# Sending a supertile's scatters as one group instead of through a paced queue, in a routed feed-forward kernel

## The chip, the cores and the metric

One Trainium2 chip, of which the kernel uses one core. Times are device microseconds (us) of one execution, from launch to end; the median over many runs is compared. The profile is one execution recorded by the hardware profiler.

## The reference

The input x holds 32 sequences of 256 tokens with 128 features, 8192 tokens in all. A modulation vector is made for each sequence from c and wmod, in six parts: shift, scale and gate for each of two halves. The two halves are:

```
h = layernorm(x) * (1 + ca) + sa
g = sigmoid(h Wg' + bg); a = sigmoid(h Wd' + bd); v = h Wv' + bv
s_t = a_t * s_(t-1) + (1 - a_t) * v_t          # scan along each sequence
x = x + ga * (s * g)

h = layernorm(x) * (1 + cb) + sb
p = softmax(h gate_w' + gate_b)                # 8 experts
y = sum over the two best experts e of p_e * (relu(h w1_e + b1_e) w2_e + b2_e)
x = x + gb * y
```

Each expert goes from 128 features to 512 and back to 128. All numbers are float32.

## The kernel before

The tokens are cut into 16 supertiles of 512 tokens (4 tiles of 128 tokens, two sequences). Each supertile passes four steps:

- `a_norm` (step 0): the first layer norm; ACT writes xn (L324).
- `a_mix` (step 1): transposes (px, L337), three matmuls of width 512 (pz, L346), the gates on ACT (ta L350, aa L352, tg L361), the scan on DVE (hs).
- `a_res` (step 2): transposes back (po, L374), the residual into xa, the second layer norm; ACT writes xm (L382).
- `a_route` (step 3): transposes (ph, L389), the logits (pl, L397), the rows back in token order (pb, L400), which ACT copies into rw (L402). DVE finds the two best experts, and a small matmul (pq, L423 and L425) counts the tokens that each expert has so far. From that DVE makes pi, the place of each of the 4 x 2 (tile, choice) pairs in a table of rows in HBM, reg. Each row has 130 words: the 128 features, the gate weight and the destination.

Eight indirect DMAs on POOL's queue (L447) write the rows of one supertile to reg, one for each pair of tile j and choice k, 128 rows each. In reg every expert has its own stretch, so that 256 rows in a row belong to one expert: a block. Reading and writing of reg is declared free of ordering between scatters, and between scatters and fills (`into_reg`).

After some supertiles (TAKE, and the last one) `table` computes on DVE which blocks are full by then: a table tb with the expert and the first row of each block. 45 blocks come from the nine tables of TAKE, the other 26 from the last table; 71 in all.

A block goes through these steps, each in another call of `b_step`:

- `b_load`: SyncE (SP) reads expert and row from tb into registers (L535, L536), loads the rows xr from reg (L538) and the expert's up-projection weights ww, 514 KB (L544). Blocks are loaded up to four ahead.
- `b_in`: two transposes (pbx, L551), and the split in a high part on ACT (xs, L553) and a low one on DVE (L554).
- `b_up`: twelve matmuls (L566 to L568) into p, and relu to hh on ACT (L574) or DVE (L572).
- `b_down`: a bias matmul (L584) and sixteen matmuls (L587) into pby, of which there is one PSUM buffer; ACT scales the result into yt (L591), eight buffers; two indirect DMAs on POOL's queue (L593) scatter it to yd.

At last `c_load` reads yd for a supertile on SP (L606), and `c_add` makes the gated sum on DVE (from L618) and stores the output (L623).

The order of the work is partly by hand. `steps` lists which steps of which supertiles stand beside each other (HEAD for the first supertiles); after each step, `between` calls `b_step` when more than BACK = 2 blocks are open and not begun. The framework's scheduler then orders the instructions of each engine, with the supertiles' steps raised in priority (AHEAD), and sets all semaphores. Each engine runs its queue in order.

In the kernel before the eight scatters of a supertile are not issued where they are made. They are appended to a list, `sending`, and `drip` takes one or two of them after each step and after each up-projection, in the order of the supertiles. Each one that is taken waits for the ACT instruction `behind`, which is the latest of the step, or the first relu of the up-projection. The blocks that a table opens are kept in `held` until the last scatter of their supertile has been taken. `b_load` has each row load wait for the last 16 scatters that were taken, and its register loads stand behind the previous block's weight load.

Of the kernel before, what the change touches and what calls it, by code (L numbers as in the profile page):

```python
# [15 lines left out]
AX = mybir.AxisListType  # L16
WAIT = mybir.DependencyInfo(mybir.DependencyClass.Sync, mybir.DependencyReason.DATA)

P = 128
# [35 lines left out]
def adaln_moe(ctx: ExitStack, tc: tile.TileContext, x, Wg, bg, Wv, bv, Wd, bd,  # L55
# [256 lines left out]
    def a_norm(s):  # L312
        g = LN1G.get(s, 0)
        if g:
            mv = wk.tile([P, g * T, 2], F32, tag=f"mva{g}", name=f"mva{s}")
            for i in range(g):
                stats(mv[:, i * T:(i + 1) * T], xa[:, s + i], f"a{s + i}")
            y, r = rsqrt(mv, f"a{s}", s)
            for i in range(g):
                ln1[s + i] = (y[:, i * T:(i + 1) * T], r[:, i * T:(i + 1) * T])  # L320
        y, r = ln1[s]
        xn = wk.tile([P, T, D], F32, tag="xn", name=f"xn{s}")
        for j in range(T):
            last = nc.scalar.activation(xn[:, j], xa[:, s, j], AF.Identity, scale=y[:, j], bias=r[:, j])  # L324
        return dict(s=s, xn=xn, last=last)

# [6 lines left out]
    def a_mix(a):  # L333
# [10 lines left out]
        for i in (2, 1, 0):  # L344
# [3 lines left out]
            if i == 2:  # L348
                ta = wk.tile([P, ST], F32, tag="ta", name=f"ta{s}")
                nc.scalar.activation(ta, z, AF.Tanh, scale=0.5, bias=hb[:, 2:3])  # L350
                aa = wk.tile([P, ST], F32, tag="aa", name=f"aa{s}")
                nc.scalar.activation(aa, ta, AF.Copy, scale=0.5, bias=0.5)  # L352
                for q in range(BPS):
                    w = slice(q * S, (q + 1) * S)
                    b = s * BPS + q
                    nc.vector.tensor_scalar(ta[:, w], ta[:, w], ngq[:, b:b + 1], gq[:, b:b + 1], op0=ALU.mult, op1=ALU.add)
            elif i == 1:
                nc.vector.scalar_tensor_tensor(ta, z, bvc, ta, op0=ALU.add, op1=ALU.mult)
            else:
                tg = wk.tile([P, ST], F32, tag="tg", name=f"tg{s}")  # L360
                a["last"] = nc.scalar.activation(tg, z, AF.Tanh, scale=0.5, bias=hb[:, 0:1])  # L361
        hs = wk.tile([P, ST], F32, tag="hs", name=f"hs{s}")
# [6 lines left out]
    def a_res(a):  # L369
# [11 lines left out]
        for j in range(T):  # L381
            a["last"] = nc.scalar.activation(xn[:, j], xt[:, j], AF.Identity, scale=y[:, j], bias=r[:, j])  # L382
        a["xn"] = xn

    def a_route(a, base):
# [13 lines left out]
        for j in range(T):  # L399
            nc.tensor.transpose(pb[:, j * P:(j + 1) * P], hT[:, j * P:(j + 1) * P], ident)  # L400
        rw = wk.tile([P, T, K, RW], F32, tag="rw", name=f"rw{s}", bufs=3)
        a["last"] = nc.scalar.activation(rw[:, :, :, 0:D], pb.rearrange("p (t d) -> p t d", d=D).unsqueeze(2).to_broadcast([P, T, K, D]), AF.Copy)  # L402
        lg = wk.tile([P, T, E], F32, tag="lg", name=f"lg{s}")
# [41 lines left out]
        nc.gpsimd.tensor_copy(rw[:, :, :, D + 1].bitcast(I32), dst[:, s * T:(s + 1) * T])  # L445
        def send(j, k):
            w = nc.gpsimd.indirect_dma_start(  # L447
                out=reg, out_offset=bass.IndirectOffsetOnAxis(ap=pi[:, j * K + k:j * K + k + 1], axis=0),
                in_=rw[:, j, k], in_offset=None)
# [7 lines left out]
    sending = []  # L457
    sent = []
    held = []
# [70 lines left out]

    loaded = []

    def b_load(n, tb, i):
        with tc.issue_after(loaded[-1].ins) if loaded else nullcontext():
            e = nc.sync.value_load(tb[i:i + 1, 0:1], min_val=0, max_val=E - 1)  # L535
            r = nc.sync.value_load(tb[i:i + 1, 1:2], min_val=0, max_val=E * CAP)  # L536
        xr = bk.tile([P, NJ, RW], F32, tag="xr", name=f"xr{n}", bufs=YTB + 6)
        w = nc.sync.dma_start(xr, reg[bass.ds(r, BLK)].rearrange("(t p) d -> p t d", p=P))  # L538
# [5 lines left out]
        loaded.append(nc.sync.dma_start(ww, wd[bass.ds(e, 1)].rearrange("o p f -> p (o f)")))  # L544
        return b
# [11 lines left out]
    def b_up(b):  # L557
        n, xs, ww = b["n"], b["xs"], b["ww"]
        hh = bk.tile([P, NH, BLK], F32, tag="hh", name=f"hh{n}")
        for k0 in range(0, NH, 2):  # L560
# [8 lines left out]
            for k in (k0, k0 + 1):  # L569
# [3 lines left out]
                else:  # L573
                    w = nc.scalar.activation(hh[:, k], p1[:, k - k0], AF.Relu, bias=bias)  # L574
                    b.setdefault("last", w)
        b["hh"] = hh
# [56 lines left out]
    def b_step():  # L633
# [23 lines left out]
    slot = 0  # L657
    alive = True

# [24 lines left out]
    for t, todo in enumerate(steps):  # L684
        def step3(s):
            nonlocal base, done
            with tc.high_priority(AHEAD[3] * (s >= EARLY)):
                base = a_route(st[s], base)
                if s in CLS:
# [3 lines left out]
                    counts.append(b)  # L693
                nb = len(blocks) + sum(len(x) for _, x in held)
                if s in TAKE:
                    n = full(s) - nb
                    tb, done = table(s, counts[:1] * (s > CUT) + [base], done, n, False)
                    held.append((s, [(tb, q, []) for q in range(n)]))
                elif s == NS - 1:
                    n = touched(s) - nb  # L700
                    tb, done = table(NS, counts, done, n, True)
                    fills(base)
                    rest = [(tb, q, []) for q in range(n)]
                    held.append((s, rest))
                    z = 0
                    for c in CLS:
                        u = max(E, touched(c) - nb) if c == CUT else touched(c) - nb
                        rest[u - 1][2].extend(range(z, c + 1))
                        z = c + 1
# [21 lines left out]
        if t == LATE:  # L731
            late_constants()
    alive = False
    while len(flow) < len(blocks) + 2 or ended or adding:
        b_step()
    assert not sending and not held

# [27 lines left out]
```

## Time and profile before

| | |
|---|---|
| median of 14 runs | 545.85 us (542.51 to 551.52) |
| the profiled execution | 549.71 us |
| its span, first to last instruction | 547.9 us |
| PE busy | 442.9 us, 2810 matmuls |
| ACT, DVE, POOL busy | 288.1, 283.3, 290.6 us |
| mean granted clock of TensorE | 0.866 |
| L447 on POOL | 128 instructions, 979 ns each |
| L593 on POOL | 142 instructions, 987 ns each |

PE is TensorE's matmuls, PEld its weight loads, DVE is VectorE, ACT ScalarE, POOL GpSimd, SP SyncE. A letter q behind the engine's name stands for its sequencer. A row of the timeline gives start, duration, engine, line, operation, the tiles written and read, how many instructions it merges, and in brackets the idle time of the engine before it and what ended it by the profile; "remote" is a semaphore whose sender the profile does not name, "issue" means that nothing it shows was waited for. A row of a stretch gives for each engine busy time and, behind x, the count of instructions. The ends of matmuls are modelled by the profiler. The granted clock is what TensorE's throttle let through, as a share of full speed.

### The profile page before, as it was taken

To read this page: it belongs to the slowest core of one execution; us is meant where nothing else is said; L and a number is where in the kernel's file an instruction comes from. 1 tells how busy PE (TensorE), PEld (TensorE's weight loads), DVE (VectorE), ACT (ScalarE), POOL (GpSimd) and SP (SyncE) were. 2 spreads that over 40 slices of the span, in tenths; PEclk is the share of its full clock that TensorE was granted. 3 is DMA by queue.
4 is the path that set the end of the run, shared out by engine and by line. 5 is a ranking of instruction groups with operands and counts; after the bars stand their busy time and mean duration, and the time that the engine had idled before them with its cause. 6 is when DMAs were issued, how large, how long until landed. Compare 5 with 4: busy or idle time off the path is not lost.

```text
span 547.9 us, 11399 instructions
## 1 busy us (share of the span) xinstructions
PE 442.9 (81%) x2810; PEld 370.7 (68%) x2810; DVE 283.3 (52%) x1511; ACT 288.1 (53%) x726; POOL 290.6 (53%) x322
## 2 busy tenths in 40 slices
PE   5668658679798799888978988776777999979991
PEld 3234415567677687756876977666676999979980
DVE  6999799568464673755547422311111220533464
ACT  4877346658555574746536533433333565636550
POOL 4537653355565566665555573666655254434451
PEclk9965586798797888988889786998979899979996
DMA  7993110826273444443442644456318676999974
GB/s 207 335 332 132 44 35 26 264 60 209 57 221 97 134 139 132 136 132 107 131 129 62 208 144 136 138 163 196 127 45 242 204 225 215 288 299 307 291 208 127
DMA packets 81845, 91.52 MB, mean 167 GB/s; under 512 B 8577, under 2 KB 66408, under 8 KB 81782
## 3 DMA queue, kind: packets, MB, share of 16 engines
q1 hardware_dynamic: 73024, 73.84, 45.9%
q0 software_dynamic: 8704, 16.94, 9.1%
q8 instruction: 26, 0.43, 0.3%
q14 instruction: 37, 0.30, 0.2%
q10 hardware_dynamic: 54, 0.02, 0.0%
HBM read 64.24 MB, written 27.43 MB: 167 GB/s over the span
## 4 chain that ended last, share of the span: by engine, by line
PE 63%; DVE 13%; issue 7%; DMA 5%; ACT 5%; another core or an unknown queue 3%; SPq 2%; POOL 1%; ACTq 0%; DVEq 0%; POOLq 0%
PE pby L587 26%; PE p L568 7%; PE p L566 6%; PE p L567 6%; PE pz L346 5%; PE pby L584 4%; PE pbx L551 3%; DVE sta L280 2%; PE pl L397 2%; DMA yk<-yd 1%; PE px L337 1%; PE po L374 1%; DVE hs L365 1%; ACT yt L591 1%
## 5 line engine op out<-in xcount | busy, mean ns | idle before, releaser
L593 POOL DMA_INDIRECT yd<-yt,xr x142 | 140.2, 987 | 141.6 <-ACT yt L591 105.8
L587 PE MATMUL pby<-wr,hh 128*128 x1136 | 167.9, 306 | 0.0
L447 POOL DMA_INDIRECT reg<-rw,pi x128 | 125.3, 979 | 76.2 <-issue 37.7
L587 PEld LDWEIGHTS pby<-wr,hh 128*128 128x128 f32 x1136 | 152.6, 214 | 10.0 <-issue 2.5
L574 ACT ACTIVATE hh<-p,ww 128x256 f32<-128x256 f32 x231 | 95.8, 480 | 39.4 <-issue 13.0
L591 ACT ACTIVATE yt<-pby,xr 128x128 f32<-128x128 f32 x142 | 44.9, 365 | 135.7 <-PE pby L587 55.7
L554 DVE TENSOR_TENSOR xs<-pbx,xs 128x256 fp32r<-128x256 f32 x71 | 30.0, 422 | 141.1 <-ACT xs L553 101.7
L566 PE MATMUL p<-xs,ww 128*128 128x256 f32 x284 | 92.2, 326 | 12.6 <-DVE hh L572 7.1
L567 PE MATMUL p<-xs,ww 128*128 128x256 f32 x284 | 83.5, 294 | 1.6 <-issue 1.5
L568 PE MATMUL p<-xs,ww 128*128 128x256 f32 x284 | 83.3, 294 | 1.5 <-issue 1.5
L566 PEld LDWEIGHTS p<-xs,ww 128*128 128x128 f32 x284 | 57.5, 203 | 14.5 <-DVE hh L572 7.9
L346 PE MATMUL pz<-h,wT 128*128 128x512 f32 x96 | 60.2, 749 | 7.0 <-ACT tg L361 4.2
L567 PEld LDWEIGHTS p<-xs,ww 128*128 128x128 f32 x284 | 57.5, 203 | 2.8 <-issue 2.8
L568 PEld LDWEIGHTS p<-xs,ww 128*128 128x128 f32 x284 | 57.0, 201 | 2.7 <-issue 2.7
L584 PE MATMUL pby<-b2w,ones_r 2*128 x71 | 28.5, 401 | 22.9 <-ACT yt L591 21.4
L584 PEld LDWEIGHTS pby<-b2w,ones_r 2*128 2x128 f32 x71 | 13.7, 193 | 41.1 <-ACT yt L591 24.8
L346 PEld LDWEIGHTS pz<-h,wT 128*128 128x128 f32 x96 | 20.2, 241 | 23.8 <-issue 10.0
L572 DVE TENSOR_SCALAR hh<-p,ww 128x256 f32<-128x256 f32 x53 | 25.4, 480 | 20.4 <-ACT hh L574 16.7
L551 PE MATMUL pbx<-ident,xr 128*128 128x128 f32 x142 | 30.5, 299 | 2.3 <-DMA xr<-reg 2.1
L553 ACT ACTIVATE xs<-pbx 128x256 fp32r<-128x256 f32 x71 | 27.5, 387 | 7.7 <-issue 2.3
L324 ACT ACTIVATE xn<-xa,nra,nya 128x128 f32<-128x128 f32 x64 | 26.5, 494 | 8.5 <-DVE nra L307 8.5
L382 ACT ACTIVATE xm<-xa,nrb,nyb 128x128 f32<-128x128 f32 x64 | 26.4, 484 | 4.4 <-DVE nrb L307 3.9
(181 smaller groups left out, 590.4 us busy)
## 6 DMA issues: line engine op xcount, KB each, us to landing
ww<-wd SPq DMA_DIRECT2D x71, 514.0 KB
xr<-reg SPq DMA_DIRECT2D x71, 130.0 KB
yk<-yd SPq DMA_DIRECT2D x30, 256.0 KB
wd<-wh SPq DMA_DIRECT2D x8, 514.0 KB
xa<-in_L_attn_x_dram SPq DMA_DIRECT2D x16, 256.0 KB
out_dram<-ot SPq DMA_DIRECT2D x15, 256.0 KB
yd<-yt,xr POOLq DMA_INDIRECT x142
w1s<-in_L_ffn_w_dram SPq DMA_DIRECT2D x8, 256.0 KB
```

What stands on the lines that cost most here:

```text
L346: nc.tensor.matmul(z, wT[:, i], h1, start=True, stop=True)
L447: w = nc.gpsimd.indirect_dma_start(out=reg, out_offset=bass.IndirectOffsetOnAxis(ap=pi[:, j * K + k:j * K + k + 1], axis=0), in_=rw[:, j, ...
L551: nc.tensor.transpose(px[:, j * P:(j + 1) * P], xr[:, j, 0:D], ident)
L554: nc.vector.tensor_tensor(xs[:, 1], px, xs[:, 0], op=ALU.subtract)
L566: nc.tensor.matmul(z, hi, xs[:, 0], start=True, stop=False)
L567: nc.tensor.matmul(z, hi, xs[:, 1], start=False, stop=False)
L568: nc.tensor.matmul(z, lo, xs[:, 0], start=False, stop=True)
L574: w = nc.scalar.activation(hh[:, k], p1[:, k - k0], AF.Relu, bias=bias)
L584: nc.tensor.matmul(py.rearrange("p (j d) -> p j d", d=D), ones_r, b2t, start=True, stop=False)
L587: nc.tensor.matmul(py[:, j * D:(j + 1) * D], hh[:, k, j * P:(j + 1) * P], we[:, k * D:(k + 1) * D], start=False, stop=(j == NJ - 1 and k = ...
L591: nc.scalar.activation(yt[:, j], py[:, j * D:(j + 1) * D], AF.Copy, scale=xr[:, j, D:D + 1])
L593: w = nc.gpsimd.indirect_dma_start(out=yd, out_offset=bass.IndirectOffsetOnAxis(ap=xr[:, j, D + 1:D + 2].bitcast(I32), axis=0), in_=yt[:, ...
```

## The change

The lists `sending`, `sent` and `held`, the function `drip` and the waits it sets are taken out. `a_route` issues its eight scatters itself, one after another. The blocks of a table go to `blocks` as soon as the table's instructions are written. A row load waits for scatters by the framework's own tracking of reg alone: for those that stand before it in the program. Its register loads may be moved ahead by the scheduler. The tiles rw and pi have two buffers instead of three. The arithmetic is the same, and so is the number of DMAs.

```diff
-        rw = wk.tile([P, T, K, RW], F32, tag="rw", name=f"rw{s}", bufs=3)
+        rw = wk.tile([P, T, K, RW], F32, tag="rw", name=f"rw{s}")
...
-        pi = wk.tile([P, T * K], I32, tag="pi", name=f"pi{s}", bufs=3)
+        pi = wk.tile([P, T * K], I32, tag="pi", name=f"pi{s}")
...
-        def send(j, k):
-            w = nc.gpsimd.indirect_dma_start(
-                out=reg, out_offset=bass.IndirectOffsetOnAxis(ap=pi[:, j * K + k:j * K + k + 1], axis=0),
-                in_=rw[:, j, k], in_offset=None)
-            into_reg(w.ins, "scat")
-            return w.ins
-
-        sending.extend((s, send, j, k) for j in range(T) for k in range(K))
+        for j in range(T):
+            for k in range(K):
+                w = nc.gpsimd.indirect_dma_start(
+                    out=reg, out_offset=bass.IndirectOffsetOnAxis(ap=pi[:, j * K + k:j * K + k + 1], axis=0),
+                    in_=rw[:, j, k], in_offset=None)
+                into_reg(w.ins, "scat")
...
-    def drip(n, behind):
-        for _ in range(min(n, len(sending))):
-            s, send, j, k = sending.pop(0)
-            w = send(j, k)
-            tc.add_manual_dep(w, behind.ins.name, WAIT, reason="pace of the rows on their way out")
-            sent.append(w)
-            if not sending or sending[0][0] != s:
-                while held and held[0][0] <= s:
-                    blocks.extend(held.pop(0)[1])
...
     def b_load(n, tb, i):
-        with tc.issue_after(loaded[-1].ins) if loaded else nullcontext():
-            e = nc.sync.value_load(tb[i:i + 1, 0:1], min_val=0, max_val=E - 1)
-            r = nc.sync.value_load(tb[i:i + 1, 1:2], min_val=0, max_val=E * CAP)
+        e = nc.sync.value_load(tb[i:i + 1, 0:1], min_val=0, max_val=E - 1)
+        r = nc.sync.value_load(tb[i:i + 1, 1:2], min_val=0, max_val=E * CAP)
...
-        for x in sent[-2 * K * T:]:
-            tc.add_manual_dep(w.ins, x.name, WAIT, reason="its rows")
...
         if i >= 1 and flow[i - 1]:
             b_up(flow[i - 1])
-            drip(1 if alive else 2, flow[i - 1]["last"])
...
-                    held.append((s, [(tb, q, []) for q in range(n)]))
+                    blocks.extend((tb, q, []) for q in range(n))
...
         for i, s in todo:
             (step0, step1, step2, step3)[i](s)
-            drip(2 if t < len(steps) - NS or len(sending) > K * T else 1, st[s]["last"])
             between()
```

More of the change, by code (lines that the diff above doesn't have):

```diff
@@ L1 @@
-from contextlib import ExitStack, nullcontext
+from contextlib import ExitStack
 import concourse.bass as bass
@@ L16 @@
 AX = mybir.AxisListType
-WAIT = mybir.DependencyInfo(mybir.DependencyClass.Sync, mybir.DependencyReason.DATA)
 P = 128
@@ L323, in a_norm @@
         for j in range(T):
-            last = nc.scalar.activation(xn[:, j], xa[:, s, j], AF.Identity, scale=y[:, j], bias=r[:, j])
-        return dict(s=s, xn=xn, last=last)
+            nc.scalar.activation(xn[:, j], xa[:, s, j], AF.Identity, scale=y[:, j], bias=r[:, j])
+        return dict(s=s, xn=xn)
     def early(s, tag, name, bufs=1):
@@ L360, in a_mix @@
                 tg = wk.tile([P, ST], F32, tag="tg", name=f"tg{s}")
-                a["last"] = nc.scalar.activation(tg, z, AF.Tanh, scale=0.5, bias=hb[:, 0:1])
+                nc.scalar.activation(tg, z, AF.Tanh, scale=0.5, bias=hb[:, 0:1])
         hs = wk.tile([P, ST], F32, tag="hs", name=f"hs{s}")
@@ L381, in a_res @@
         for j in range(T):
-            a["last"] = nc.scalar.activation(xn[:, j], xt[:, j], AF.Identity, scale=y[:, j], bias=r[:, j])
+            nc.scalar.activation(xn[:, j], xt[:, j], AF.Identity, scale=y[:, j], bias=r[:, j])
         a["xn"] = xn
@@ L400, in a_route @@
             nc.tensor.transpose(pb[:, j * P:(j + 1) * P], hT[:, j * P:(j + 1) * P], ident)
-        rw = wk.tile([P, T, K, RW], F32, tag="rw", name=f"rw{s}", bufs=3)
-        a["last"] = nc.scalar.activation(rw[:, :, :, 0:D], pb.rearrange("p (t d) -> p t d", d=D).unsqueeze(2).to_broadcast([P, T, K, D]), AF.Copy)
+        rw = wk.tile([P, T, K, RW], F32, tag="rw", name=f"rw{s}")
+        nc.scalar.activation(rw[:, :, :, 0:D], pb.rearrange("p (t d) -> p t d", d=D).unsqueeze(2).to_broadcast([P, T, K, D]), AF.Copy)
         lg = wk.tile([P, T, E], F32, tag="lg", name=f"lg{s}")
@@ L445, in a_route @@
         nc.gpsimd.tensor_copy(rw[:, :, :, D + 1].bitcast(I32), dst[:, s * T:(s + 1) * T])
-        def send(j, k):
-            w = nc.gpsimd.indirect_dma_start(
-                out=reg, out_offset=bass.IndirectOffsetOnAxis(ap=pi[:, j * K + k:j * K + k + 1], axis=0),
-                in_=rw[:, j, k], in_offset=None)
-            into_reg(w.ins, "scat")
-            return w.ins
-        sending.extend((s, send, j, k) for j in range(T) for k in range(K))
-        return rk[:, T]
-    sending = []
-    sent = []
-    held = []
-    def drip(n, behind):
-        for _ in range(min(n, len(sending))):
-            s, send, j, k = sending.pop(0)
-            w = send(j, k)
-            tc.add_manual_dep(w, behind.ins.name, WAIT, reason="pace of the rows on their way out")
-            sent.append(w)
-            if not sending or sending[0][0] != s:
-                while held and held[0][0] <= s:
-                    blocks.extend(held.pop(0)[1])
+        for j in range(T):
[4 more added lines that the diff above has]
+                into_reg(w.ins, "scat")
+        return rk[:, T]
     def table(i, counts, done, n, last):
@@ L528, in fills @@
             into_reg(w.ins, "fill")
-    loaded = []
     def b_load(n, tb, i):
-        with tc.issue_after(loaded[-1].ins) if loaded else nullcontext():
-            e = nc.sync.value_load(tb[i:i + 1, 0:1], min_val=0, max_val=E - 1)
-            r = nc.sync.value_load(tb[i:i + 1, 1:2], min_val=0, max_val=E * CAP)
+        e = nc.sync.value_load(tb[i:i + 1, 0:1], min_val=0, max_val=E - 1)
+        r = nc.sync.value_load(tb[i:i + 1, 1:2], min_val=0, max_val=E * CAP)
         xr = bk.tile([P, NJ, RW], F32, tag="xr", name=f"xr{n}", bufs=YTB + 6)
@@ L539, in b_load @@
         tc.add_to_no_dep_group("rows", w.ins)
-        for x in sent[-2 * K * T:]:
-            tc.add_manual_dep(w.ins, x.name, WAIT, reason="its rows")
         ww = bk.tile([P, WW], F32, tag="ww", name=f"ww{n}", bufs=5)
         b = dict(n=n, xr=xr, ww=ww, tb=tb, i=i)
-        loaded.append(nc.sync.dma_start(ww, wd[bass.ds(e, 1)].rearrange("o p f -> p (o f)")))
+        nc.sync.dma_start(ww, wd[bass.ds(e, 1)].rearrange("o p f -> p (o f)"))
         return b
@@ L573, in b_up @@
                 else:
-                    w = nc.scalar.activation(hh[:, k], p1[:, k - k0], AF.Relu, bias=bias)
-                    b.setdefault("last", w)
+                    nc.scalar.activation(hh[:, k], p1[:, k - k0], AF.Relu, bias=bias)
         b["hh"] = hh
@@ L657, in adaln_moe @@
     slot = 0
-    alive = True
     def between():
@@ L693, in step3 @@
                     counts.append(b)
-                nb = len(blocks) + sum(len(x) for _, x in held)
+                nb = len(blocks)
                 if s in TAKE:
@@ L702, in step3 @@
                     fills(base)
-                    rest = [(tb, q, []) for q in range(n)]
-                    held.append((s, rest))
+                    blocks.extend((tb, q, []) for q in range(n))
                     z = 0
@@ L707, in step3 @@
                         u = max(E, touched(c) - nb) if c == CUT else touched(c) - nb
-                        rest[u - 1][2].extend(range(z, c + 1))
+                        blocks[nb + u - 1][2].extend(range(z, c + 1))
                         z = c + 1
@@ L732, in adaln_moe @@
             late_constants()
-    alive = False
     while len(flow) < len(blocks) + 2 or ended or adding:
         b_step()
-    assert not sending and not held
 _INS = ['L0_attn_x', 'L0_attn_Wg', 'L0_attn_bg', 'L0_attn_Wv', 'L0_attn_bv', 'L0_attn_Wd', 'L0_attn_bd',
```

## The prediction

> **What bounds the kernel now.** I read the page first, then busy time by stretch, then the queues of POOL, ACT and PE against each other, then SyncE's waits. The page:
>
> ```profile
> PE 442.9 (81%) x2810; PEld 370.7 (68%) x2810; DVE 283.3 (52%) x1511; ACT 288.1 (53%) x726; POOL 290.6 (53%) x322
> ```
>
> TensorE is the busiest engine, so the question is where it loses time. Busy time by stretch (PE, PEld, DVE, ACT, POOL, granted TensorE clock, DMA share, GB/s):
>
> ```profile
> 100.00:343.00 243.00, 210.19 (x1339) 179.88 (x1340) 132.21 (x760) 137.47 (x349) 138.73 (x148) 0.86 0.45 138
> 343.00:425.00 82.00, 60.88 (x434) 54.98 (x433) 14.36 (x50) 28.94 (x81) 49.51 (x52) 0.93 0.52 153
> 425.00:535.00 110.00, 106.51 (x820) 99.25 (x819) 41.52 (x86) 60.88 (x171) 49.00 (x50) 0.96 0.85 255
> ```
>
> From 100 to 343 us three blocks run for each supertile; at 343 the last supertile is routed; to 425 the queue still drips its last 21 scatters; after 425 there are blocks alone, and TensorE is full: one block each 3.95 us (block 46 ends at 434.2, block 58 at 481.7). Up to 425 it is idle for 32.8 + 21.1 = 54 us, and the granted clock takes (1 - 0.86) x 243 + (1 - 0.93) x 82 = 40 us more: 94 us in all. The timeline shows what goes with it. POOL, then ACT, then PE, near 395 us:
>
> ```profile
> 392.20 0.99 POOL L593 DMA_INDIRECT yd<-yt,xr  x1 [0.30 <-ACT hh L574]
> 393.49 0.98 POOL L593 DMA_INDIRECT yd<-yt,xr  x1 [0.30 <-issue]
> 394.77 0.96 POOL L447 DMA_INDIRECT reg<-rw,pi  x1 [0.30 <-issue]
> 396.04 0.96 POOL L447 DMA_INDIRECT reg<-rw,pi  x1 [0.30 <-issue]
> ```
> ```profile
> 398.32 0.62 ACT L591 ACTIVATE yt<-pby,xr 128x128 f32<-128x128 f32 x2 [6.33 <-remote]
> ```
> ```profile
> 391.52 2.05 PE L587 MATMUL pby<-wr,hh 128*128 x16
> 399.00 0.58 PE L584 MATMUL pby<-b2w,ones_r 2*128 x1 [3.79 <-ACT yt L591]
> 399.51 3.78 PE L587 MATMUL pby<-wr,hh 128*128 x16
> ```
>
> The matmuls that ACT's yt reads end at 393.6 by the profile, yet yt starts at 398.3, 1.3 us after POOL finished a run of six indirect DMAs without a break (389.7 to 397.0). I call time from the recorded end of what an engine waits for to its start a stall. Nearly all of them between 100 and 425 us end 0.8 to 1.4 us after an indirect DMA, mostly the last of a run. By the length of the run, pieces within 0.45 us of each other, the stall per run is 1.2 us (three DMAs, 12 runs), 1.7 (four, 6), 2.8 (five, 7), 4.5 (six, 5), 5.1 (seven, 5) and 4.1 (eight, 1); pairs show 1.1. They sum to 106 us. This is a correlation, and the profile does not show what TensorE is held by; 94 us lost for 106 us of stall makes 0.9 us lost for one stalled.
>
> **The change, part by part.** *Scatters together.* Nothing is removed from POOL: 128 row scatters and 142 scatters of results remain, about 0.98 us each and 1.27 from start to start. What moves is their order. In the changed program POOL's queue holds the eight L447 scatters of a supertile as one piece, mostly with a pair of L593 before and after it and other pairs further on; now it holds one to three L447 between pairs. A run of eight lasts 8 x 1.27 = 10.2 us. Between runs of four and seven the stall grows by (5.1 - 1.7) / 3 = 1.1 us a DMA. I take runs of nine, eight scatters with a pair touching them half the time: 5.1 + 2 x 1.1 = 7.3 us, plus 2.5 pairs x 0.9 = 2.2: 9.5 us a supertile. Supertiles 3 to 15 have their scatters between 85 us and the end of routing: 13 x 9.5 = 124, with 5 us for the pairs of six further blocks 129, against 106 now: 23 x 0.9 = **+20 us**. Bounds: eight alone 6.2 + 2.7 = 8.9 gives 121, +13; twelve in a run 10.7 + 1.8 = 12.5 gives 168, +55. Downwards the nearest rows disagree, and they carry the main rival below.
>
> [...]
>
> *Blocks open at their table.* In SyncE's queue the load of a block's rows still waits for scatters, but of a supertile that is complete, and in steady state of rows sent a supertile earlier. What is removed is this wait (SyncE's own queue):
>
> ```profile
> SPq L538 <- DMA reg<-rw,pi: 72.4, 17, 15.7
> ```
>
> Most of it is hidden: block 33's rows are asked for at 315.9 and used at 341.8. It shows once: the row loads stand still from 386.9 to 410.3, until supertile 15's last drip has left, and TensorE waits about 2 us near 421: **-2 us**. The table reads of a later supertile now stand before weight loads of earlier blocks in SyncE's queue (weights of block 12 behind table 5, say). These blocks are used about one and a half supertiles (some 35 us) after that table, which hides it; without that cover it would be one wait for a table per supertile, 1 to 3 us.
>
> *Head.* POOL now sends 8, then 6, then 7 scatters, with the last three of the first 24 at 90.3 to 93.8; block 0's rows are asked for at 95.4. In the changed order all 24 stand one after another: the third supertile's eight start when sixteen have left, at about 70.5, and end near 81. Block 0 can start some 13 us earlier, on a TensorE busy for 12.8 of the 20 us from 80 to 100 while VectorE is busy for 19.3. By the order of instructions 33 instead of 31 blocks are finished when supertile 15 is routed. Two blocks fewer after that are worth 2 x 3.95 = **-8 us** (bounds -11, all three early blocks in idle time, and -4, half given back to the VectorE-bound supertiles). Running blocks there delays supertile 3 and 4 on PE, 1.4 us of up-projection each time, which VectorE's queue hides.
>
> *Smaller edits.* rw and pi go from three buffers to two: the scatters that read a buffer now leave some 13 us after routing, and the buffer is rewritten two supertiles (47 us) later, so nothing; without that cover ACT would hold rw at L402. The waits of each scatter on an ACT instruction go; POOL's eight then wait for pi, and pairs of L593 stand behind them for up to 10.2 us. Eight yt buffers at 4 us a block hold 32 us of results, so ACT does not wait. Scatters' landings and all arithmetic stay.
>
> Sum: +20 - 2 - 8 = +10 us on the profiled execution, 549.7 us (span 547.9 plus 1.8 around it), which is 0.7% above the median of 14 runs, 545.85. The same +10 on the median gives **556 us**.
>
> **Rivals.** 1. *Faster: the stall does not grow with the run.* Speaking for it: runs of six to eight cost 4.5, 5.1 and 4.1, flat within their scatter. With 4.7 us a run the total is 13 x (4.7 + 2.7) + 5 = 101, -5 x 0.9 - 10 = -14: **531 us**. The purest rows go further, the runs of scatters alone in the head:
>
> ```profile
> 47.23 1.23 POOL L447 DMA_INDIRECT reg<-rw,pi  x1 [0.32 <-DVE mva L282]
> ...
> 56.38 1.13 POOL L447 DMA_INDIRECT reg<-rw,pi  x1 [0.30 <-issue]
> ```
> ```profile
> 53.47 1.02 ACT L402 ACTIVATE rw<-pb 128x1024 f32<-128x1024 f32 x1 [0.40 <-PE pq L425]
> 54.39 0.68 ACT L361 ACTIVATE tg<-pz,hb 128x512 f32<-128x512 f32 x1
> ```
>
> Six and seven microseconds into eight scatters, ACT still takes TensorE's results at once; the three head runs show 0.5, 2.3 and 0 us. Were that so beside blocks, the total would be 13 x 3.6 + 5 = 52, and -49 - 10 gives 487 us, the far end. Against it: in the head TensorE has only supertile work and SyncE loads no blocks, and beyond 5 us into a run between 100 and 425 us stalls fill over 80% of the time. I would put real weight on 500 to 531. It decides at a stall below about 6 us for each run of eight.
>
> 2. *No change that can be told.* The cost per run lands where +0.9 x added stall equals 10 us, 117 us in all, 8.6 a supertile: a run stall of 6 us. A window of 3.2 us around the old median is narrow beside these uncertainties.
>
> 3. *Slower by much: everything queues up.* Pairs that come ready during the eight follow at once, runs become twelve and the sum is +55 - 10 = +45: **591 us**. Against it: a stalled TensorE yields no new results to scatter.
>
> 4. *The early opening does nothing*, because rows now come behind bursts and head blocks wait for weights: then -8 is lost and the likeliest case becomes 564.
>
> **How the numbers follow.** A measurement tells 0.3%, 1.6 us, from no change. Slower (likeliest, with rivals 3 and 4): 0.55; faster (rival 1): 0.38; same: 0.07. The likeliest case's own range, from runs of eight with full head gain (548) to eleven or twelve in a run, is 548 to 580. Cases of both signs hold much of the chance, so the range reaches down to 512, leaving out the far end of rival 1 and the 591 of rival 3: 512 to 580.
>
> **What would show it.** Right: in the timeline, runs of eight or more L447 with ACT idle for 6 to 8 us ending about 1.3 us after them, once a supertile; the granted clock between 100 and 343 us at or below 0.86; PE busy share there lower than 210 of 243; and PE full, at 3.95 us a block, as soon as the last run has passed. Wrong: ACT taking matmul results during the second half of these runs, supertile intervals under the present 23.5 us, or the tail from routing to end (now 204 us) shorter by 20 us with no longer middle. The first L538 near 82 us instead of 95.4 would confirm the head part alone.

## The result and the profile after

The changed kernel takes 593.72 us (median of 10 runs, 589.81 to 601.5), against 545.98 us for the kernel before (47 runs): a ratio of 1.087, 95% interval 1.084 to 1.090. It is slower by 48 us where +10 was forecast; the direction was right, and the time lies above the stated 512 to 580 us. The profiled execution took 597.69 us, its span is 596.0 us, 48.1 more than before.

The same two kernels, measured again in one other session (a session is one chip that runs a few kernels one after another, always with the kernel before beside them), gave a ratio of 0.958, 0.952 to 0.965. Both results stand. The experiments show what differs; this section reads the recorded pair. Lines of the changed kernel are numbered up to 24 lower: L538 is now L517, L544 L521, L591 L567, L593 L569, L587 L563; L447 has kept its number.

TensorE, in the page of the kernel after, does the same work (PE, PEld, DVE, ACT, POOL, with busy share and instructions):

```profile
PE 445.0 (75%) x2810; PEld 371.0 (62%) x2810; DVE 287.1 (48%) x1511; ACT 290.1 (49%) x726; POOL 290.4 (49%) x322
```

Not one engine is busier by more than 4 us; the 48 us are waiting. To place them I cut both traces where the count of supertile 3 (pq, before at 87 us, after at 105) and that of supertile 15 (344 and 416) run on TensorE. Busy time by stretch, columns as before, first of the kernel before:

```profile
40.00:87.00 47.00, 31.76 (x107) 17.77 (x108) 42.75 (x304) 24.60 (x53) 26.47 (x28) 0.65 0.19 71
87.00:344.00 257.00, 219.94 (x1387) 186.27 (x1386) 145.03 (x862) 147.59 (x370) 146.77 (x158) 0.85 0.45 135
```

and of the kernel after:

```profile
43.00:105.00 62.00, 36.23 (x133) 22.06 (x133) 43.89 (x306) 27.33 (x58) 26.18 (x29) 0.63 0.28 97
105.00:416.00 311.00, 227.80 (x1415) 192.07 (x1414) 145.14 (x838) 147.80 (x369) 158.76 (x171) 0.81 0.35 108
```

Supertile 3 comes 18 us later (what of this is waiting stands under "The unchanged kernels"), the twelve supertiles after it take 311 instead of 257 us (+54), and from the last routing to the end it is 180 instead of 204 us (-24). 18 + 54 - 24 = 48. In the middle TensorE does nearly the same number of matmuls, at a granted clock of 0.81 instead of 0.85.

One run of the changed kernel shows what happens. POOL, then ACT, then PE of the kernel after, near 214 us (start, duration, engine, line, operation, tiles, and in brackets the idle time before):

```profile
213.93 0.96 POOL L447 DMA_INDIRECT reg<-rw,pi  x1 [0.50 <-issue]
...
222.77 0.96 POOL L447 DMA_INDIRECT reg<-rw,pi  x1 [0.30 <-issue]
```
```profile
225.59 0.62 ACT L567 ACTIVATE yt<-pby,xr 128x128 f32<-128x128 f32 x2 [10.64 <-remote]
```
```profile
211.98 2.05 PE L563 MATMUL pby<-wr,hh 128*128 x16
...
226.77 3.57 PE L563 MATMUL pby<-wr,hh 128*128 x15
```

The result that yt reads is finished at 214.0 by the profile. ACT gets it at 225.6, after all eight scatters have passed, and 1.9 us after the last ended. The matmuls that follow run at 3.57 us for fifteen instead of 2.05 for sixteen. By the prediction's measure of a stall (from the recorded end of what is waited for to the start), the thirteen long runs of supertiles 3 to 15 cost 7.8 to 12.5 us each, 10.8 us on average (ACT's rows alone give 8.4 to 13.2 and 11.0, so such figures are good to about a microsecond); eight of them are ten DMAs long, three twelve, two eight.

### The profile page after: what moved, and what is told of

The parts are those of the page before. It is cut to its first block, busy times and chain, and to the rows that moved or that the text cites. A ratio compares the mean times of both kernels' runs of the same rounds, so it can differ in the third digit from the quotient of the medians.

```text
span 596.0 us, 11368 instructions
## 1 busy us (share of the span) xinstructions
PE 445.0 (75%) x2810; PEld 371.0 (62%) x2810; DVE 287.1 (48%) x1511; ACT 290.1 (49%) x726; POOL 290.4 (49%) x322
## 4 chain that ended last, share of the span: by engine, by line
PE 52%; another core or an unknown queue 15%; DVE 14%; issue 9%; DMA 4%; ACT 4%; SPq 1%; POOL 0%; ACTq 0%; POOLq 0%; DVEq 0%
PE pby L563 20%; PE p L543 5%; PE p L544 5%; PE p L545 5%; PE pz L345 4%; PE pby L560 3%; PE pbx L528 2%; PE pl L396 2%; DMA xa<-in_L_attn_x_dram 2%; DMA yk<-yd 1%; PE ph L388 1%; DMA yd<-yt,xr 1%; DVE hs L364 1%; DVE sta L279 1%
## 5 line engine op out<-in xcount | busy, mean ns | idle before, releaser
L569 POOL DMA_INDIRECT yd<-yt,xr x142 | 141.9, 1000 | 193.7 <-ACT yt L567 134.1
L563 PE MATMUL pby<-wr,hh 128*128 x1136 | 167.6, 301 | 16.9 <-issue 16.9
L563 PEld LDWEIGHTS pby<-wr,hh 128*128 128x128 f32 x1136 | 149.9, 209 | 28.3 <-issue 20.4
L447 POOL DMA_INDIRECT reg<-rw,pi x128 | 123.5, 965 | 74.1 <-issue 34.8
L567 ACT ACTIVATE yt<-pby,xr 128x128 f32<-128x128 f32 x142 | 44.8, 363 | 139.2 <-remote 66.6
L544 PE MATMUL p<-xs,ww 128*128 128x256 f32 x284 | 84.6, 298 | 7.1 <-issue 7.1
L345 PE MATMUL pz<-h,wT 128*128 128x512 f32 x96 | 58.7, 727 | 24.8 <-DVE ta L357 17.1
L543 PEld LDWEIGHTS p<-xs,ww 128*128 128x128 f32 x284 | 58.4, 206 | 9.0 <-DVE hh L549 4.5
L545 PEld LDWEIGHTS p<-xs,ww 128*128 128x128 f32 x284 | 58.1, 205 | 7.3 <-issue 7.3
L544 PEld LDWEIGHTS p<-xs,ww 128*128 128x128 f32 x284 | 58.6, 206 | 5.9 <-issue 5.9
L345 PEld LDWEIGHTS pz<-h,wT 128*128 128x128 f32 x96 | 19.0, 226 | 41.9 <-issue 32.2
L381 ACT ACTIVATE xm<-xa,nrb,nyb 128x128 f32<-128x128 f32 x64 | 26.5, 483 | 21.0 <-remote 11.3
L375 DVE TENSOR_TENSOR xa<-po,xa 128x512 f32<-128x512 f32 x16 | 11.0, 689 | 45.2 <-remote 34.1
```

Of the source, the lines that this page charges most:

```text
L345: nc.tensor.matmul(z, wT[:, i], h1, start=True, stop=True)
L447: w = nc.gpsimd.indirect_dma_start(out=reg, out_offset=bass.IndirectOffsetOnAxis(ap=pi[:, j * K + k:j * K + k + 1], axis=0), in_=rw[:, j, ...
L543: nc.tensor.matmul(z, hi, xs[:, 0], start=True, stop=False)
L544: nc.tensor.matmul(z, hi, xs[:, 1], start=False, stop=False)
L545: nc.tensor.matmul(z, lo, xs[:, 0], start=False, stop=True)
L563: nc.tensor.matmul(py[:, j * D:(j + 1) * D], hh[:, k, j * P:(j + 1) * P], we[:, k * D:(k + 1) * D], start=False, stop=(j == NJ - 1 and k = ...
```

## The experiments

Eight sessions ran fourteen kernels. In four of them the kernel before took 473.65, 474.95, 476.33 and 473.86 us, in the other four 541 to 547, 548.96, 550.03 and 544.85. From e7 on each kernel ran once in its session. I call what makes the difference the hold: time in which results are finished by the profile and not taken until a run of indirect DMAs has passed. My theory at the start was that a long run holds TensorE's results in proportion to its length. The rivals: the early opening costs, the third buffer was needed, or TensorE's own register load of the expert is what stands still.

### Grouping, opening, buffers, register load

`e1`, the kernel before with all eight at once (the head and the held blocks stay):

```
-            drip(1 if alive else 2, flow[i - 1]["last"])
+            drip(8, flow[i - 1]["last"])
...
-            drip(2 if t < len(steps) - NS or len(sending) > K * T else 1, st[s]["last"])
+            drip(8, st[s]["last"])
```

> Before, with the queue, the held blocks and the three buffers kept, but all eight scatters of a supertile taken from the queue at once. Theory (a long run of indirect DMAs on POOL holds TensorE's results for nearly its whole length, about 10 us for each run of ten): the grouping alone carries the loss, 590 to 606 us, and the early opening is worth only a few us either way. Rival (the early opening costs, by row loads that wait in SyncE's queue and by blocks put ahead of the first supertiles): 545 to 560 us, near the kernel before.

`e2` is the same with 4 in both places.

> Before, with four scatters taken from the queue at once instead of one or two. Theory: two runs of four to six for each supertile, some 3 us held in each, 13 x 2 x 3 = 78 to 110 us held in all against 106 before: 540 to 560 us. Rival (any grouping that lets POOL's pairs wait costs in proportion): half of the loss, about 570 us.

`e3` is the kernel after with `bufs=3` for rw and pi.

> After, with three buffers again for rw and pi. Theory: nothing, 592 to 596 us, since the scatters have left long before a buffer is written again. Rival (the two buffers hold ACT or VectorE, and so the supertiles): 550 to 580 us.

`e4`, the kernel after with TensorE's register load left out:

```
-        e = nc.tensor.value_load(b["tb"][i:i + 1, 0:1], min_val=0, max_val=E - 1)
-        we = wr[:, bass.ds(e, 1), :].rearrange("p o f -> p (o f)")
-        b2t = b2w[:, bass.ds(e, 1), :].to_broadcast([2, NJ, D])
+        we = wr[:, 0]
+        b2t = b2w[:, 0:1, :].to_broadcast([2, NJ, D])
```

> After, with TensorE's register load of the expert left out: every block is multiplied with the down-projection and the bias of expert 0, so the output is not the reference's. Theory A (TensorE's results are held by the run itself, whatever TensorE does): 588 to 596 us. Rival B (a register load in TensorE's queue, which stands still while POOL writes descriptors, is what holds the results behind it): the runs cost next to nothing, 490 to 520 us.

Measured beside a kernel before of 473.65 us: e1 461.38 (ratio 0.973, 0.968 to 0.978), e2 463.92 (0.979, 0.974 to 0.984), e3 453.66 (0.956, 0.952 to 0.961), e4 457.27 (0.963, 0.959 to 0.968). None of the expectations had a place for this: all four are faster than before (e2 by about 2%), and the kernel before itself is 72 us faster than recorded. So these four say nothing of the hold, and the unchanged kernels were run again.

### The unchanged kernels

> The changed kernel itself, unchanged, beside the kernel before once more. In the last four runs the kernel before took 473.65 us instead of 546, and no run of indirect DMAs held TensorE's results at all. Theory A (whether POOL's runs hold TensorE is a property of the chip that a run lands on, not of the kernel): where before takes about 474 us, after takes 452 to 460 us, ratio 0.955 to 0.97, as with three buffers; where before takes about 546 us, after takes 588 to 600, ratio 1.08 to 1.09. Theory B (the third buffer or the pacing, not the chip, took the hold away): after is at 588 to 600 us whatever before takes.

> The kernel before, unchanged, for its own profile outside the first recording. Theory A (the hold is a property of the chip): either 470 to 480 us with no pause of ACT or VectorE behind finished matmuls at POOL's runs, clock 0.91 to 0.92, or 541 to 552 us with the 106 us held between 100 and 425 us. Nothing between. If it is the first, the same queue of instructions runs with a supertile interval near 18 us instead of 23.5, POOL has hardly a gap in it, and what bounds it is read from this profile.

e5 took 455.44 us beside 474.95, ratio 0.958 (0.952 to 0.965), without the third buffer. e7, in another session, took 541.48 us, with 106 us of stall between 100 and 425 us as in the first recording. Theory B of e5 falls: neither pacing nor buffer removes the hold. The other half of theory A, that it belongs to the chip, fell later: the chip that the record numbers 8 ran e1 to e4 without a hold and e12 with it.

What a session without the hold looks like, in e5. POOL and ACT around one group of eight:

```profile
219.93 0.96 POOL L447 DMA_INDIRECT reg<-rw,pi  x1 [0.30 <-issue]
...
228.76 0.96 POOL L447 DMA_INDIRECT reg<-rw,pi  x1 [0.30 <-DMA reg<-rw,pi]
```
```profile
225.14 0.35 ACT L567 ACTIVATE yt<-pby,xr 128x128 f32<-128x128 f32 x1
229.10 0.62 ACT L567 ACTIVATE yt<-pby,xr 128x128 f32<-128x128 f32 x2 [0.96 <-PE pby L563]
```

POOL's DMAs take the same 0.96 us, and ACT takes a block's result in the middle of the run. From 95 to 217 us there stand 94 indirect DMAs in one run, and ACT takes every result at once. A stretch of e5:

```profile
93.00:280.00 187.00, 185.50 (x1415) 161.08 (x1413) 144.63 (x833) 145.32 (x365) 142.93 (x153) 1.00 0.57 174
```

TensorE is busy for 185.5 of 187 us at full clock. The gain there has two parts, which e1 and e3 separate in one session: grouping alone gives 2.7% (461.38 against 473.65), and the early opening, with the waits that go with it, 1.7% more (453.66). SyncE's row loads wait for scatters in e5 for 51.3 us in all, in e1 for 67.2, in e6 below, which has the queue of before, for 150.9.

These sessions also show what the new order costs by itself in the head. The count of supertile 3, first in e6, then in e5, of the same session:

```profile
83.94 0.19 PE L440 MATMUL pq<-mk,tri 128*128 128x40 bf16 x1 [1.24 <-DVE mk L437]
```
```profile
92.54 0.18 PE L422 MATMUL pq<-mk,tri 128*128 128x40 bf16 x1
```

It is 8.6 us later with the scatters together, though nothing is held. (In e1, which keeps the held blocks, it stands at 93.4.) Since the count of supertile 2 TensorE has run 75 matmuls in e5 and 46 in e6, a block's up-projection and part of another supertile's mix among them, and VectorE 192 instructions against 162. So, by the difference between these sessions and the recorded pair, about half of the 18 us is order, and the rest is hold.

### Probes among blocks alone

`e6` adds two groups of eight indirect DMAs to the end of the kernel before, into a table of their own:

```
+            w = nc.gpsimd.indirect_dma_start(
+                out=dump, out_offset=bass.IndirectOffsetOnAxis(ap=dumpi[:, q:q + 1], axis=0),
+                in_=pad[:, 0], in_offset=None)
...
+            extra(EXTRAS.get(i - 1, 0), flow[i - 1]["last"])      # {46: 8, 56: 8}
```

> Before, with sixteen extra indirect DMAs of 128 rows into a table that nobody reads, in two groups of eight, behind the first relu of blocks 46 and 56, where TensorE has blocks alone. Theory A: on a chip where before takes about 546 us each group holds TensorE's results for some 10 us, 560 to 570 us in all; on one where it takes about 474 us POOL hides them, 474 to 480 us. Theory B (the hold needs the supertiles' steps on TensorE beside the run): nothing on either, within 4 us of before.

473.62 us beside 474.95, ratio 0.998 (0.995 to 1.002): without the hold, sixteen more DMAs cost nothing. To meet a session with the hold, e1, e4 and e6 were run again:

> The kernel of e1 (groups of eight, held blocks, three buffers) once more, for a chip on which POOL's runs hold TensorE. If before takes 541 to 552 us beside it: theory (the grouping alone carries the loss) 590 to 610 us; rival (the early opening carries it) 541 to 560 us. If before takes about 474 us: 461 us, as in e1.

> The kernel of e4 (after, without TensorE's register load of the expert, all blocks with expert 0 in the down-projection) once more. If before takes 541 to 552 us beside it: theory A (the runs hold TensorE's results whatever its queue holds) 585 to 600 us; rival B (the register load is what is held, and everything behind it) 455 to 490 us. If before takes about 474 us: 457 us, as in e4.

> The kernel of e6 (before, with two groups of eight extra indirect DMAs among blocks alone) once more. If before takes 541 to 552 us beside it: theory A (a long run holds TensorE wherever it stands) 560 to 570 us, two holds of some 10 us; rival B (the hold needs the supertiles' steps) within 6 us of before. If before takes about 474 us: within 4 us of it, as in e6.

They met one without: 461.76, 456.95 and 475.32 us beside 476.33, as the first time. So the questions went into one kernel, e1 with four probes, and with expert 0 and no register load in blocks 15 to 26:

```
+EXTRAS = {46: ("indirect", 8), 54: ("SP", 8), 59: ("compute", 2), 64: ("indirect", 4)}
+STATIC = (15, 27)
```

> The kernel of e1 (groups of eight, held blocks, three buffers) with four probes among the blocks alone at the end: eight extra indirect DMAs behind block 46, eight plain DMAs of the same 66 KB on SyncE's queue behind block 54, two VectorE-like subtractions of 2048 words on POOL (some 10 us without a DMA) behind block 59, four extra indirect DMAs behind block 64. Blocks 15 to 26 use expert 0 in the down-projection and no register load on TensorE, so the output is not the reference's. On a chip where before takes 541 to 552 us: theory A (the run of indirect DMAs itself holds TensorE) the runs in the middle hold some 10 us each with and without the register load, the eight at block 46 hold 8 to 10 us, the four at block 64 1 to 3 us, the plain DMAs and the compute nothing; supertile 15 is routed at 405 to 420 us as in the changed kernel. Theory B (the register load) no holds while blocks 15 to 26 run. Theory C (early opening carries the loss, not the grouping) supertile 15 is routed near 345 us. Theory D (DMA traffic in general) the plain DMAs hold as much as the indirect ones. On a chip where before takes about 474 us nothing holds anywhere and the whole takes 465 to 485 us.

> The kernel of e11 once more, for a chip on which POOL's runs hold TensorE, with the same expectations: there, by theory A, supertile 15 is routed at 405 to 420 us, the runs of eight to ten in the middle hold some 10 us each with and without TensorE's register load (blocks 15 to 26), the eight extra indirect DMAs at block 46 hold 8 to 10 us, the four at block 64 1 to 3 us, the plain DMAs and the compute nothing; by theory B the holds are missing while blocks 15 to 26 run; by theory C supertile 15 is routed near 345 us. Where before takes about 474 us: 466 us, as in e11.

e11 took 466.16 us beside 473.86, with no hold. e12 took 612.28 beside 548.96, and answers:

- Supertile 15 is routed at 415 us, in the kernel after at 416, in the one before at 344. The blocks are held in e12. Supertile 3 is routed at 105 us, as in the kernel after. So the grouping carries the loss up to there, and the early opening adds nothing to it that can be seen: theory C falls.
- While blocks 15 to 26 are at work the runs of ten hold 10.6, 8.2, 11.5 and 11.3 us, elsewhere 9.1 to 10.8. The register load is not the cause: theory B falls.
- Among blocks alone the eight extra DMAs, with four of L593 (here L622) that queued behind them, hold as much as in the middle. The hold does not need supertile steps.

The count of supertile 15, in the kernel after and in e12:

```profile
416.30 0.21 PE L422 MATMUL pq<-mk,tri 128*128 128x40 bf16 x1 [5.52 <-DVE mk L419]
```
```profile
415.05 0.21 PE L448 MATMUL pq<-mk,tri 128*128 128x40 bf16 x1 [5.88 <-DVE mk L445]
```

POOL, ACT and SyncE of e12 at the probes (L284 and L288 are the extras, L620 is yt; the x3, x1 and x4 on SyncE are eight plain DMAs):

```profile
475.11 0.96 POOL L284 DMA_INDIRECT dump<-pad,dumpi  x1 [1.42 <-ACT yt L620]
...
489.12 0.97 POOL L622 DMA_INDIRECT yd<-yt,xr  x1 [0.30 <-issue]
```
```profile
485.20 0.63 ACT L620 ACTIVATE yt<-pby,xr 128x128 f32<-128x128 f32 x2 [7.99 <-remote]
492.39 1.20 ACT L599 ACTIVATE hh<-p,ww 128x256 f32<-128x256 f32 x3 [6.28 <-issue]
...
522.30 0.63 ACT L620 ACTIVATE yt<-pby,xr 128x128 f32<-128x128 f32 x2 [1.37 <-PE pby L616]
```
```profile
515.94 1.31 SPq L288 DMA_DIRECT2D dump<-pad  x3
...
517.90 0.43 SPq L288 DMA_DIRECT2D dump<-pad  x1
...
521.01 2.66 SPq L288 DMA_DIRECT2D dump<-pad  x4
```

During the eight plain DMAs on SyncE (515.9 to 523.7) yt comes every 3.92 us as ever. During the two subtractions on POOL nothing is held either; they took 3.62 us each with a pair of L622 between them, not the 10 us that were planned, so ten unbroken microseconds of computing were not tried. The four indirect extras, for which 1 to 3 us were expected, came in a run of six and hold 5.4 us.

`e13` has groups of four in the middle and extras broken by pauses:

> Before, with four scatters taken from the queue at once, and among the blocks alone at the end sixteen extra indirect DMAs: eight behind block 46 with a POOL subtraction of 256 words (some 0.6 us without a DMA) after each, eight behind block 56 with one of 640 words (some 1.2 us) after every second one. Where before takes 541 to 552 us: theory A (results are held from 2 to 4 us into an unbroken run to 1.4 us after its end, so that the price is the run's length less some 3 us, and any pause ends it) runs of four to six in the middle hold 2 to 5 us each, supertile 15 is routed at 350 to 385 us, between 344 in the kernel before and 415 with eight at once, and the extras with pauses hold under 1 us for each piece. Theory B (it is the rate of DMAs over some ten us, not the break, that holds) the extras with pauses hold nearly as much as the eight without, 6 us or more for each group of eight. Where before takes about 474 us no hold anywhere, 465 to 480 us.

600.22 us beside 550.03. Supertile 15 is routed at 396 us, later than expected but in order: 344 with one or two, 396 with four, 415 with eight. Runs of six hold 4.9 us on average, of eight 7.2, of twelve 12.0 (by ACT's rows alone 4.3, 7.0 and 11.4); two calls of the queue often met and made eight. In the first group of extras each pause is 0.65 us long, which makes 0.8 us between two DMAs. Results get through in between, but from 469 to 515 us the pieces hold about 15 us together, up to 3.7 each. ACT's yt before and after:

```profile
468.55 0.63 ACT L616 ACTIVATE yt<-pby,xr 128x128 f32<-128x128 f32 x2 [0.27 <-PE pby L612]
...
516.23 0.64 ACT L616 ACTIVATE yt<-pby,xr 128x128 f32<-128x128 f32 x2
```

These ten blocks take 47.7 us, 8.4 more than at 3.93 us each; in e12, with the eight extras in one run, four blocks took 28.0 us (yt at 474.7 and at 502.7), 12.3 more. So the last part of theory A, under 1 us for each piece, falls, and theory B's own sign, 6 us or more for a group of eight, is met: with gaps of 0.8 us between two DMAs the group still held. With 1.67 us between the pairs of L593 (L622) at the end of e12 nothing was held: from 443 to 475 us yt comes every 3.9 us. The second group came out unlike its plan, its first five extras without a long pause, in a run of four and a run of five. Behind 528 us its pieces of two and three DMAs, with up to 1.5 us between them, let ACT wait 1.0 us at most.

`e14` asks what it is in the DMAs:

```
+                w = nc.gpsimd.dma_start(dump[q * P:(q + 1) * P], pad[:, 0])        # block 48, plain
...
+                    out=dump, out_offset=bass.IndirectOffsetOnAxis(ap=dumpi[0:16, q:q + 1], axis=0),
+                    in_=pad[0:16, 0], in_offset=None)                               # block 58, 16 rows
```

> Before, unchanged up to the last routing, with two probes among the blocks alone: eight plain DMAs of 128 rows of 520 bytes to fixed places, issued by POOL, behind block 48, and eight indirect DMAs of 16 rows instead of 128 behind block 58. Where before takes 541 to 552 us: theory A (it is POOL writing descriptors, indirect or not) the eight plain DMAs hold 8 us or more, as eight indirect ones did; theory B (only the indirect form holds) they hold under 2 us. For the small ones: theory C (the price goes by the rows) they hold under 3 us; theory D (it goes by the DMAs and their completions) 8 us or more. Where before takes about 474 us nothing holds, 470 to 478 us.

551.29 us beside 544.85, a session with the hold. POOL and ACT (L281 plain, L283 indirect with 16 rows, L611 is yt):

```profile
430.50 4.38 POOL L281 DMA_DIRECT2D dump<-pad  x8
...
471.29 0.87 POOL L283 DMA_INDIRECT dump<-pad,dumpi  x1 [0.30 <-issue]
...
479.40 0.84 POOL L283 DMA_INDIRECT dump<-pad,dumpi  x1 [0.30 <-issue]
```
```profile
431.35 0.63 ACT L611 ACTIVATE yt<-pby,xr 128x128 f32<-128x128 f32 x2 [1.45 <-PE pby L607]
435.29 0.63 ACT L611 ACTIVATE yt<-pby,xr 128x128 f32<-128x128 f32 x2 [1.45 <-PE pby L607]
...
482.90 0.63 ACT L611 ACTIVATE yt<-pby,xr 128x128 f32<-128x128 f32 x2 [12.25 <-remote]
```

Eight plain DMAs of the same bytes on POOL, in 4.4 us and next to pairs on both sides, hold nothing: yt comes 3.94 us after the last. The pairs that they put back then stand four in a row from 438.4 to 443.2 us, and behind these ACT waits 2.5 us. The plain ones went through the same DMA queue as the indirect ones, by the bytes of this queue in the kernel before and in e14 (0.60 MB more: eight plain DMAs are 0.53, the small ones 0.07):

```profile
q0 software_dynamic: 8704, 16.94, 9.1%
```
```profile
q0 software_dynamic: 9216, 17.54, 9.3%
```

Eight indirect ones with an eighth of the rows, in a run of ten with the pair before them, hold 9.5 us and leave ACT idle for 12.25. Theories B and D stand: it is the indirect form, and the price goes by the DMAs and hardly by the rows. Whether it goes by their number or by the time they take is not separated, since one of 16 rows takes nearly as long as one of 128; and a plain run of ten microseconds on POOL was not tried.

## Why the prediction was wrong

The path was the right one: in the recorded session runs of indirect DMAs hold results, and longer runs hold more. Two terms of the sum failed: the stall of a run with the eight scatters (7.3 us; 10.8 measured), and the 24 scatters of the head, whose stall was put at nothing and whose reordering was to be hidden (supertile 3 came 18 us later). With the measured 153 us of stall the prediction's own sum behind the head is (153 - 106) x 0.9 - 2 - 8 = +32, against the +30 that was measured there; the head's 18 us are the rest of the 48.

*The size of a run (+20; by the measured stalls +42).* The prediction took nine DMAs at 7.3 us. The runs are mostly ten, and hold 10.8. The growth from four to seven was read well enough: a hold lasts to between 1 and 2.4 us after the run, whatever its length, so one more DMA adds its own 1.27 us, against the 1.1 taken. What failed is the anchor, 5.1 us at seven. In the kernel before, a run gets long because pairs of L593 join it, and a pair can join only if TensorE's results have come through. The long runs of before are thus those in which the hold set in late: by ACT's rows the first result that waits is 3.7 to 7.2 us into the runs of seven. In the kernel after the eight stand there without asking TensorE, and the first result waits 0.7 to 6.0 us into the run, 2.8 on average. A run of ten lasts 12.5 us, and ACT's waits reach from 2.9 us into it to 2.0 us after it on average: 11.6 us, of which 10.4 are held. These rows fit the argument; no run tests the selection by itself. Pairs by themselves were priced too high, 0.9 us against 0.27. In sum the stalls from supertile 3 to the end of the last group are 153 us where 129 were forecast and 106 stood before.

*The head (its stall put at nothing; supertile 3 in fact 18 us later).* This was the larger miss for its size. About half of it is order: as e5 and e6 show, the work that now runs ahead of supertile 3 puts it back by 8.6 us even where nothing is held, where the prediction had 1.4 us of up-projection each time, hidden by VectorE's queue. The rest is hold. The prediction let the scatters of the second and third supertile stand in one run of sixteen at no cost, since runs of six to eight in the head had cost 0.5, 2.3 and 0 us. It holds 14.5 us. And it holds more than TensorE. VectorE of the kernel after in that run, on instructions that read VectorE's own results alone:

```profile
73.76 0.16 DVE L306 SCALAR_TENSOR_TENSOR nrb<-mvb,nyb 128x4 f32<-128x4 f32 x1 [1.22 <-issue]
75.18 0.17 DVE L300 TENSOR_TENSOR nta<-nta,nva 128x4 f32<-128x4 f32 x1 [1.26 <-DVE nrb L306]
79.39 0.16 DVE L301 SCALAR_TENSOR_TENSOR nta<-nta 128x4 f32<-128x4 f32 x1 [4.05 <-remote]
```

and the same two steps in e5, in the same run of sixteen without the hold:

```profile
67.46 0.15 DVE L300 TENSOR_TENSOR nta<-nta,nva 128x4 f32<-128x4 f32 x1
67.65 0.16 DVE L301 SCALAR_TENSOR_TENSOR nta<-nta 128x4 f32<-128x4 f32 x1
```

VectorE goes about one step per DMA (1.2 to 1.3 us idle before each), and later none for 4 us; without the hold a step takes 0.2 us. So the name "TensorE's results" in the prediction was too narrow, and runs of six to eight in the head did not speak for one of sixteen. Why the head's first run of eight, 10 us long, holds nearly nothing in either kernel is open. Rows did reach the blocks early, as forecast: the first row load went at 85.0 instead of 95.4 us.

*The blocks gained and SyncE's wait (-8 and -2).* 33 blocks are done when supertile 15 is routed, 31 before: this held. After it 24 us are saved: two blocks, 8 us, and 21 us less of stalls (10.6 against 31.8), not all of which shortened the chain. The wait of the row loads for scatters is gone from SyncE's rows; in its place the wait of the weight loads has grown, from 41.0 us in the kernel before. SyncE's own queue in the kernel after:

```profile
SPq L521 <- DVE hh L549: 115.7, 23, 14.6
```

*The buffers.* Nothing was forecast. In e5 ACT does wait for a buffer of rw at L401, for 15.9 us in all behind scatters of reg, and in e3, with three buffers, for 1.1 us; the time shows nearly none of it. No session measured the third buffer against two in the same run; 453.66 and 455.44 us in two sessions of the same kind leave no room for more than some 2 us.

*The clock.* The prediction's sum has no term of its own for it: 40 us of granted clock stand in the 94 us behind its 0.9 us lost for one stalled. In the kernel after, behind the holds that end near 170, 226, 416 and 436 us, a block's sixteen matmuls take 3.62 to 3.78 us instead of 2.05. By the prediction's own count the clock took (1 - 0.81) x 311 = 59 us between supertiles 3 and 15, against (1 - 0.85) x 257 = 39 before; how much of these 20 us goes with the holds is not shown. In the head six matmuls pz took 5.46 us after 16.5 us of idle PE, where two took 1.12 us at 68.9 us.

*The rivals.* Rival 3 forecast 591 us, near the result, by runs of twelve; three of thirteen were. Its number came near by luck: the head and the early hold made up for the shorter runs. Rival 1, a stall of no account, is what every session without the hold shows, to its far end: there the kernel before itself is 72 us faster, and the change gains 4.2% on top. The prediction took the stall as a property of the kernel; one profile could not show that it comes and goes with the session.

*What stays open.* Nothing here shows what switches the hold on. It was the same for all kernels of a session and differed between sessions, also between two on the chip numbered 8. One observation goes with it: the records of semaphore updates in the trace. In the first 40 us, before the first indirect scatter, there are about 1,000 in every run. In whole runs there are 11,108 in e5 and 11,161 in e1, and only 6,192 in the recorded run of the kernel after, 6,145 in e12 and 6,142 in e14. They go missing beside the runs: from 60 to 80 us, in the run of sixteen, the kernel after keeps 66 and e5 386, though the engines also did less there; from 50 to 60 us, in the first run of eight, which holds nearly nothing, 69 and 193. Records that go missing and results that are taken late could have one cause; that is a guess, which no run here tests. Every execution here left a span and a clock on record, so none tells, either, whether the hold exists where nothing is recorded.

Regrouping was not tried further for sessions with the hold. With 14 indirect DMAs of 1.27 us in a supertile of 23.5 us, 5.7 us are left for gaps; in e13 gaps of 0.8 us were too short and 1.67 us between the pairs of e12 were enough, so some four runs of three or four are about the most that fit. At 1.2 to 1.7 us of stall each, as in the kernel before, that is about 6 us a supertile, an estimate from these rows; the kernel before has some 75 us in twelve, which is as much. Without the hold the kernel after, with two or three buffers, is the fastest of all that ran.

## What to carry to other kernels

Price a queue of one engine by the longest unbroken run that it may form, and look for the price in runs that do not depend on the results they would hold up: here the runs of seven that TensorE's own results had fed held 5.1 us, and the thirteen runs of eight to twelve in the kernel after held 10.8 us on average, though no run tests the selection by itself. Before a stall without a visible cause is built into a forecast, run the unchanged kernel again in other sessions; here one and the same change was worth +8.7% or -4.2%. With the hold the paced queue was the faster form here, 545.98 us against 593.72 (0.8 us between two DMAs was too little to end a hold, 1.67 us between pairs enough); without it grouping was 2 to 3% faster than pacing (e2 463.92 and e1 461.38 us against 473.65).

## What the runs showed of the hardware

- In the recorded session and those of e7 and e12 to e14 the other engines did not go on with finished results during unbroken runs of indirect DMAs on POOL: in the kernel after from 0.7 to 6.0 us into a run to between 1 and 2.4 us after it, 10.8 us on average over thirteen runs. Mostly these were TensorE's results; in its run of sixteen VectorE's own waited too, 4.05 us at the longest. In e5 94 in a row held nothing.
- The price went by the DMAs and hardly by the rows: eight with 16 rows each, behind two of 128, held 9.5 us in a run of 11.5 (e14); twelve with 128 rows held 12.0 in a run of 15.0 (e13). Eight plain DMAs of 128 rows on POOL (4.4 us, e14) or on SyncE (7.8 us, e12), and 3.6 us of computing on POOL (e12), held nothing.
- An indirect DMA of 16 rows took POOL 0.84 us (e14), one of 128 rows 0.96: so the rows were a small part of its time. A plain DMA took POOL 0.55 (4.38 us for eight, e14).
